# A two-layer graph attention kernel: transposes of the layer input in odd steps, layer-0 sums counted behind V, mask tiles of the first batch turned inside the stream

## Chip, cores and metric

The kernel runs on one core of one Trainium2 chip. The metric is the device time of one execution in microseconds, as the median of several runs.

## What is computed

`x` is 16 x 1024 x 256 in float32, `adj` is 16 x 1024 x 1024 in int32 (0 or 1). Two layers follow each other, each a pre-norm graph attention with a residual; layer 0 has 4 heads of 64, layer 1 has 8 heads of 32 and biases. Cut to what matters:

```python
for layer in (0, 1):                       # H = 4, then 8; D = 256 // H
    h = relu(layernorm(x))
    q, k, v = h @ Wq, h @ Wk, h @ Wv       # per head; layer 1 with bq, bk, bv
    s = q @ k.T / sqrt(D)                  # per batch and head, 1024 x 1024
    s = where(adj, s, -inf)
    x = x + concat_heads(softmax(s) @ v) @ Wo + bo
```

## The kernel before

All matmuls are float32. Keys lie on the 128 partitions of a score tile and 512 queries on its columns. A *group* is one batch, one layer, one half of the queries (`qh`) and one half of the heads (`g`: 2 heads in layer 0, 4 in layer 1). A *step* makes four 128x512 score blocks of a group: two key tiles of two heads in layer 0 (4 steps a group), one key tile of four heads in layer 1 (8 steps a group). A batch so has 16 layer-0 steps and 32 layer-1 steps.

All steps of all batches form one list, and layer 0 of batch b+1 stands ahead of layer 1 of batch b. In step i of this list (`Stream.run`, L436) TensorE gets the scores of step i (`scores`, L356, into two PSUM pairs `ps`), then the products with V of step i-2 (`weigh`, L389, into `po`; `LEAD` is 2). VectorE sets masked scores to a large negative number (L380) and ScalarE takes the exponential (L385). The pool `ps_s` has three PSUM pairs; a step's scores take two of them in turn, and every projection, transpose or output product takes one.

The sums of the exponentials come from a matmul with ones (`count`, L268, into `pz`). In layer 1 GpSimd first adds the tiles of two steps (L482) and the count is put into step i+2. In layer 0 VectorE and GpSimd add the tiles of a group (`add_tiles`, L401) and one count follows at its end. Then `spread` (L285) copies the sums out of PSUM on ScalarE and re-lays them by two DMAs through DRAM (`sd`, `sn`), `invert` (L294) takes the reciprocal on VectorE and brings it back broadcast (`vd`, `inv`), `test` (L306) checks the range of the sums on GpSimd, `normalize` (L313) multiplies on GpSimd, and `end_half` (L340) multiplies with Wo and adds to x.

The inputs of the next layers are made in between, in pieces placed by hand: `later(i, f)` puts a function into step i, `due` holds them, and they are issued at the end of the step in the order in which they were entered. The pieces are `stats` and `norm` (mean and variance on VectorE, normalized rows `hn` on ScalarE), `add_bias`, `turn` (L189, eight TensorE transposes of `hn` to `hT`), and `k`, `q`, `values`. `k`, `q`, `values` and `end_half` are the *large* units (L428). An even step that has a large unit holds its products with V back, and the next odd step does those of both.

The mask of a batch comes in eight tiles: `load` (GpSimd's DMA queue, which also turns int32 to bf16), `flip` (SyncE's transposing DMA), `put` (ScalarE, to fp8), with two buffers before and two behind the flip. The second layer's form of the mask is made in place by `second` (L136, VectorE). In the first batch all eight tiles are put ahead of the stream. SyncE's queue (SP) issues all other DMAs in program order.

For the batches in the middle, with a the first layer-0 step of a 48-step cycle and c = a+16 its first layer-1 step, the placing is (each named unit for one half of 512 rows):

| unit | before |
|---|---|
| k, q, v and k of the coming layer-1 batch | a+2, a+4, a+6, a+8 |
| its remaining v and q | c+2, c+4 |
| turns of the coming layer-1 batch | c+28, c+30 |
| turn, k, q, v of the next layer-0 batch, half 0 | a+14, c+6, c+10, c+12 |
| the same, half 1 | c+14, c+16, c+18, c+20 |
| output products of layer 0 | c, c+8 |
| output products of layer 1 | c+26, a+10 |

Of the kernel before, what the change touches and what calls it, by code (L numbers as in the profile page):

```python
# [18 lines left out]
P = 128  # L19
# [3 lines left out]
LEAD = 2  # L23

# [15 lines left out]
def load_weights(nc, const, a):  # L40
# [19 lines left out]
    for layer in range(2):  # L60
        for kind, mats in (("k", w.k), ("q", w.q), ("v", w.v), ("o", w.o)):
            mats.append(mat(a[f"w{kind}{layer}"], f"w{kind}{layer}"))
# [3 lines left out]
    w.bv = col(a["bv1"], "bv1")  # L66
    w.ident = const.tile([P, P], F32, tag="ident", name="ident")
# [8 lines left out]
def fast_program(ctx, tc, a, w, loads, chk):  # L76
# [26 lines left out]

    bo = [w.bo[0]]
# [39 lines left out]
    class Inputs:  # L144
# [37 lines left out]
        def add_bias(self, half):  # L182

            rows = xs[self.b, half]
            nc.gpsimd.tensor_add(
                rows, rows, bo[self.layer].unsqueeze(1).to_broadcast([P, 4, E])
            )
# [58 lines left out]
    class Group:  # L246
# [21 lines left out]
        def count(self, p, start, stop):  # L268
# [3 lines left out]
            for r in range(self.per):  # L272
# [3 lines left out]
                )  # L276

# [93 lines left out]
    def exponentials(st, between):  # L371
# [5 lines left out]
        for i in range(2):  # L377
# [8 lines left out]
            if i == 0:  # L386
                between()
# [32 lines left out]
    class Stream:  # L420
# [7 lines left out]
        def large(self, i):  # L428
            return any(
                f.__name__ in ("k", "q", "values", "end_half") for f, _ in self.due.get(i, [])  # L430
            )

        def later(self, i, f, *args):
            self.due.setdefault(i, []).append((f, args))

        def run(self):  # L436
# [3 lines left out]
            for i in range(n + LEAD):  # L440
# [5 lines left out]
                copy = lambda: None  # L446
                if i % 2 or not self.large(i):
                    for st in waiting:
                        weigh(st)
                    for st in waiting:  # L450
                        if st.gr.layer:
                            self.count_steps(i, st)
                        if st.last:
                            copy = st.gr.copy_out
                            self.end_group(i, st.gr)
                    waiting = []
                if now:
                    exponentials(now, copy)
                else:
                    copy()  # L460
# [3 lines left out]
                for f, args in self.due.pop(i, []):  # L464
                    f(*args)
# [25 lines left out]
        def end_group(self, i, gr):  # L491

            if gr.layer == 0:
                i += 1
                self.later(i, gr.count, gr.t, True, True)
            elif not gr.hurry:
                i += 2
            self.later(i, gr.spread)
            if gr.hurry:
                self.later(i, gr.finish)  # L500
                self.later(i, gr.test)
                return
            self.later(i + 2, gr.invert)
            self.later(i + 3, gr.test)

            self.later(i + (5 if gr.layer and not gr.last else 4), gr.normalize)
            if gr.g == 1:
                self.later(i + (7 if gr.layer else 6), gr.end_half)
# [19 lines left out]
    def tiles(*ts):  # L528
        for t in ts:
            mask.flip(t)  # L530
            (mask if t + 2 < NT else masks[1]).load((t + 2) % NT)
            open_w(-(-len(loads) // 2))

    tiles(0, 1)
# [62 lines left out]
    for t in range(NT):  # L597
        later(2 * t, masks[1].flip, t)
        later(2 * t + 1, masks[1].put, t)
# [296 lines left out]
```

## Time and profile before

| | |
|---|---|
| median of 3 runs | 3406.17 us (3405.55 to 3406.78) |
| profiled execution | 3402.26 us, its span 3400.5 us |
| granted TensorE clock | 0.996 of full speed |
| busy: PE, DVE, ACT, POOL | 3359.3, 2468.8, 2188.1, 2446.0 us |
| scores L364, V L396, count L273 | 1167.4, 989.9 and 267.8 us of PE |
| masking L380, exponentials L385 | 1801.3 us of DVE, 1618.2 us of ACT |
| layer-1 tile adds L482 | 1163.0 us of POOL |
| DMA | 141.76 MB, 42 GB/s in the mean |

Busy times of engines run side by side, so they do not add up to the span. A TensorE row of the timeline joins the matmuls of one line; its second column runs to a modelled end, and the distance from the start of one row to the start of the next says how long TensorE really spent on it.

### The profile page before, as it was taken

How to read it: one execution, taken by the hardware profiler on the slowest of the kernel's cores; microseconds unless marked ns; L12 is line 12 of the kernel's file. 1: busy time of each engine (PE TensorE's matmuls, PEld its weight loads, DVE VectorE, ACT ScalarE, POOL GpSimd, SP SyncE). 2: the span in 40 equal slices, each digit the busy share in tenths (PEclk: the TensorE clock that was granted, in tenths of full speed). 3: DMA queues.
4: the chain of work that ended last, by engine and by line, in shares of the span. 5: the costliest groups of instructions: out<-in, count | busy, mean ns of one | idle time of the engine just before them, and what ended most of it. 6: DMA issues, size and time to landing. Idle time of an engine off the chain costs nothing. (4 is left out here: it accounts for less than half of the span.)

```text
span 3400.5 us, 46245 instructions
## 1 busy us (share of the span) xinstructions
PE 3359.3 (99%) x18190; PEld 1302.6 (38%) x18190; DVE 2468.8 (73%) x2664; ACT 2188.1 (64%) x2402; POOL 2446.0 (72%) x1606
## 2 busy tenths in 40 slices
PE   7999999999999999999999999999999999999998
PEld 3443343433434333343333334334343343433432
DVE  4676767777677776777767777677776777767876
ACT  5566666676666756667566675666756667565665
POOL 4577777777777776777668686686867768677777
PEclk9999999999999999999999999999999999999999
DMA  6212121211212122121111212112122111210001
GB/s 133 44 36 36 47 42 36 49 37 47 40 36 51 34 49 36 36 51 42 42 35 39 48 42 45 34 43 45 39 48 39 42 41 41 47 35 23 14 17 31
DMA packets 250737, 141.76 MB, mean 42 GB/s; under 512 B 182416, under 2 KB 217488, under 8 KB 250512
## 3 DMA queue, kind: packets, MB, share of 16 engines
q1 hardware_dynamic: 232080, 105.18, 12.6%
q0 software_dynamic: 18432, 33.56, 6.4%
q8 instruction: 144, 2.36, 0.3%
q14 instruction: 81, 0.66, 0.1%
HBM read 120.33 MB, written 18.34 MB: 41 GB/s over the span
## 5 line engine op out<-in xcount | busy, mean ns | idle before, releaser
L380 DVE SCALAR_TENSOR_TENSOR p<-mask,ps 128x1024 f32<-128x1024 fp8e4 x1536 | 1801.3, 1215 | 753.7 <-PE ps L364 729.1
L385 ACT ACTIVATE p<-p 128x1024 f32<-128x1024 f32 x1536 | 1618.2, 1057 | 984.1 <-DVE p L380 940.9
L482 POOL TENSOR_TENSOR p<-p,p 128x2048 f32<-128x2048 f32 x255 | 1163.0, 4562 | 399.9 <-PE po L396 396.1
L364 PE MATMUL ps<-qT,kT 32*128 32x512 f32 (+1 forms) x6144 | 1167.4, 633 | 13.1 <-DVE p L380 8.7
L396 PE MATMUL po<-p,v 128*32 128x512 f32 (+1 forms) x6144 | 989.9, 601 | 0.5 <-ACT o L280 0.5
L409 POOL TENSOR_TENSOR t<-t,t 128x1024 f32<-128x1024 f32 x192 | 479.1, 2495 | 401.3 <-DVE t L407 324.4
L364 PEld LDWEIGHTS ps<-qT,kT 32*128 32x128 f32 (+1 forms) x6144 | 375.0, 184 | 726.2 <-issue 364.0
L396 PEld LDWEIGHTS po<-p,v 128*32 128x32 f32 (+1 forms) x6144 | 229.1, 118 | 688.3 <-issue 529.3
L407 DVE TENSOR_TENSOR t<-p 128x1024 f32<-128x1024 f32 x192 | 292.7, 1525 | 0.9
L273 PE MATMUL pz<-p,ones 128*32 128x512 f32 x2056 | 267.8, 593 | 0.2 <-POOL p L482 0.2
L207 PE MATMUL pq<-hT,wk 128*128 128x512 f32 x512 | 240.0, 612 | 2.7 <-ACT hT L196 2.6
L236 PE MATMUL pv<-wv,hT 128*128 128x256 f32 x1024 | 237.9, 385 | 0.0
L345 PE MATMUL py<-wo,cat 128*128 128x256 f32 x1008 | 234.2, 385 | 2.5 <-DVE p L380 2.5
L207 PE MATMUL pq<-hT,wq 128*128 128x512 f32 x512 | 236.6, 605 | 0.0
L236 PEld LDWEIGHTS pv<-wv,hT 128*128 128x128 f32 x1024 | 189.4, 190 | 70.7 <-issue 36.1
L345 PEld LDWEIGHTS py<-wo,cat 128*128 128x128 f32 x1008 | 186.4, 190 | 73.2 <-issue 32.3
L316 POOL TENSOR_TENSOR cat<-o,inv 128x512 f32<-128x512 f32 x127 | 164.3, 1294 | 20.7 <-DMA inv<-vd 14.7
L407 POOL TENSOR_TENSOR t<-p 128x1024 f32<-128x1024 f32 x64 | 171.5, 2680 | 0.4
L131 ACT ACTIVATE mask<-adjT,mhalf 128x1024 fp8e4<-128x1024 bf16 x128 | 145.5, 1138 | 10.1 <-DMA adjT<-adj 10.1
L207 PEld LDWEIGHTS pq<-hT,wk 128*128 128x128 f32 x512 | 93.3, 192 | 144.3 <-issue 137.1
L207 PEld LDWEIGHTS pq<-hT,wq 128*128 128x128 f32 x512 | 92.1, 189 | 139.8 <-issue 128.5
L177 ACT ACTIVATE hn<-x,shift,rstd 128x256 f32<-128x256 f32 x256 | 138.1, 588 | 6.9 <-POOL shift L170 6.9
(52 smaller groups left out, 1567.8 us busy)
## 6 DMA issues: line engine op xcount, KB each, us to landing
adj<-in_adj_dram POOLq DMA_DIRECT2D x128, 256.0 KB, 3.6
x<-in_x_dram SPq DMA_DIRECT2D x32, 512.0 KB
inv<-vd SPq DMA_DIRECT2D x128, 128.0 KB
inv<-vd SPq DMA_DIRECT2D x252, 64.0 KB
out_dram<-x SPq DMA_DIRECT2D x31, 512.0 KB
adjT<-adj SPq DMA_TRANSPOSE x128
sd<-s SPq DMA_DIRECT2D x64, 4.0 KB
sn<-sd SPq DMA_DIRECT2D x64, 4.0 KB
```

The lines of the kernel that those rows point to most:

```text
L207: nc.tensor.matmul(pq[:, m, :], wt[self.layer][:, c, ts(m, P)], self.hT[half][:, c, :], start=(c == 0), stop=(c == 1),)
L236: nc.tensor.matmul(pv[:, i, :], self.hT[half][:, c, ts(i, P)], w.v[self.layer][:, c, :], start=(c == 0), stop=(c == 1),)
L273: nc.tensor.matmul(self.s[r * self.D : (r + 1) * self.D, :], w.ones[:, : self.D], p[:, r, :], start=start, stop=stop,)
L316: nc.gpsimd.tensor_mul(self.half.cat[:, self.g, :], self.ob, self.inv)
L345: nc.tensor.matmul(py[:, i, :], self.half.cat[:, c, ts(i, P)], w.o[self.layer][:, c, :], start=(c == 0), stop=(c == 1),)
L364: nc.tensor.matmul(st.ps[i // 2][:, i % 2, :], gr.inp.kT[r * D : (r + 1) * D, gr.g, ts(kt, P)], gr.inp.qT[r * D : (r + 1) * D, gr.g, ts(gr ...
L380: nc.vector.scalar_tensor_tensor(out=half, in0=gr.mask.m[:, kt, ts(gr.qh, 512)].unsqueeze(1).to_broadcast([P, 2, 512]), scalar=BIG, in1=st ...
L385: nc.scalar.activation(half, half, AF.Exp, scale=gr.scale)
L396: nc.tensor.matmul(gr.o[r * D : (r + 1) * D, :], gr.inp.v[:, kt, h * D : (h + 1) * D], st.p[:, i, :], start=(kt == 0), stop=(kt == NT - 1),)
L407: engine.tensor_add(t, st.p[:, 0:2, :], st.p[:, 2:4, :])
L409: nc.gpsimd.tensor_add(t, t, gr.t)
L482: nc.gpsimd.tensor_add(one, one, st.p)
```

## The change

- `turn` of the layer inputs goes from even to odd steps wherever layer 1 is running (c+14 to c+15, c+28 to c+27, c+30 to c+29).
- Counts are issued directly behind the products with V, ahead of the step's other units. The layer-0 count and `spread` are due one step later than before, `invert` stays, and for a batch's last layer-1 group `invert`, `normalize` and `end_half` come one, two and one steps earlier.
- Units due in one step are sorted: small ones first, turns and large units last.
- Large units are placed anew: v and q of the coming layer-1 batch at c+4 and c+6; k, q, v of the next layer-0 batch at c+10, c+12, c+14 (half 0) and c+18, c+20, c+24 (half 1); the second layer-1 output product at a+9.
- The prologue puts four mask tiles of the first batch; the other four, and then those of batch 1, are flipped and put one per step, from steps 1 and 2 on.
- x of batch 1 is loaded between the first mask tiles; x of later batches, half 1, at a+10 for a+11. Weights of layer 1 are loaded after those of layer 0 and the biases.
- The product of bv and Wo (`pb`) moves from the prologue to step 9 and is added in place to the bias row, which also serves the second program (taken only where a sum leaves its range).

```diff
@@ -22,6 +22,9 @@
 LEAD = 2
+LARGE = ("k", "q", "values", "end_half")
+COUNTS = ("count", "count_added")
 SUM_MIN, SUM_MAX = 1e-15, 1e15
@@ -57,13 +60,17 @@
         return t
     w.k, w.q, w.v, w.o = [], [], [], []
-    for layer in range(2):
-        for kind, mats in (("k", w.k), ("q", w.q), ("v", w.v), ("o", w.o)):
-            mats.append(mat(a[f"w{kind}{layer}"], f"w{kind}{layer}"))
+    def mats(layer):
+        for kind, of in (("k", w.k), ("q", w.q), ("v", w.v), ("o", w.o)):
+            of.append(mat(a[f"w{kind}{layer}"], f"w{kind}{layer}"))
+    mats(0)
     w.bo = [row(a["bo0"], "bo0"), row(a["bo1"], "bo1")]
     w.bq = col(a["bq1"], "bq1")
     w.bk = col(a["bk1"], "bk1")
     w.bv = col(a["bv1"], "bv1")
+    mats(1)
     w.ident = const.tile([P, P], F32, tag="ident", name="ident")
     make_identity(nc, w.ident)
     w.ones = const.tile([P, 64], F32, tag="ones", name="ones")
@@ -275,6 +280,9 @@
                     start=start, stop=stop,
                 )
+        def count_added(self):
+            self.count(self.t, True, True)
         def copy_out(self):
             self.ob = work.tile([P, 512], F32, tag="o", name=f"o_{self.n}")
             nc.scalar.copy(self.ob, self.o)
@@ -427,11 +436,15 @@
         def large(self, i):
             return any(
-                f.__name__ in ("k", "q", "values", "end_half") for f, _ in self.due.get(i, [])
+                f.__name__ in LARGE for f, _ in self.due.get(i, [])
             )
         def later(self, i, f, *args):
             self.due.setdefault(i, []).append((f, args))
+        def rank(self, entry):
+            return entry[0].__name__ in ("turn", *LARGE)
         def run(self):
             steps = self.steps
@@ -443,7 +456,7 @@
                     waiting.append(steps[i - LEAD])
                 if now:
                     scores(now)
-                copy = lambda: None
+                copies = []
                 if i % 2 or not self.large(i):
                     for st in waiting:
                         weigh(st)
@@ -451,18 +464,25 @@
                         if st.gr.layer:
                             self.count_steps(i, st)
                         if st.last:
-                            copy = st.gr.copy_out
+                            copies.append(st.gr.copy_out)
                             self.end_group(i, st.gr)
                     waiting = []
+                due = self.due.pop(i, [])
+                for f, args in due:
+                    if f.__name__ in COUNTS:
+                        f(*args)
                 if now:
-                    exponentials(now, copy)
+                    exponentials(now, copies)
                 else:
-                    copy()
+                    for f in copies:
+                        f()
                 one = steps[i - 1] if 1 <= i <= n else None
                 if one and one.gr.layer == 0:
                     add_tiles(one)
-                for f, args in self.due.pop(i, []):
-                    f(*args)
+                for f, args in sorted(due, key=self.rank):
+                    if f.__name__ not in COUNTS:
+                        f(*args)
             while self.due:
                 for f, args in self.due.pop(min(self.due)):
                     f(*args)
@@ -490,22 +510,21 @@
         def end_group(self, i, gr):
+            if gr.hurry:
+                for f in (gr.spread, gr.finish, gr.test):
+                    self.later(i, f)
+                return
             if gr.layer == 0:
-                i += 1
-                self.later(i, gr.count, gr.t, True, True)
-            elif not gr.hurry:
-                i += 2
-            self.later(i, gr.spread)
-            if gr.hurry:
-                self.later(i, gr.finish)
-                self.later(i, gr.test)
-                return
-            self.later(i + 2, gr.invert)
-            self.later(i + 3, gr.test)
-            self.later(i + (5 if gr.layer and not gr.last else 4), gr.normalize)
+                self.later(i + 2, gr.count_added)
+                at = 2, 3, 5, 7
+            else:
+                at = (2, 3, 4, 8) if gr.last else (2, 4, 7, 9)
+            for k, f in zip(at, (gr.spread, gr.invert, gr.normalize)):
+                self.later(i + k, f)
+            self.later(i + at[1] + 1, gr.test)
             if gr.g == 1:
-                self.later(i + (7 if gr.layer else 6), gr.end_half)
+                self.later(i + at[3], gr.end_half)
     def open_w(n):
         for _ in range(n):
@@ -525,46 +544,48 @@
     inp.stats(1)
     inp.turn(0)
-    def tiles(*ts):
-        for t in ts:
-            mask.flip(t)
-            (mask if t + 2 < NT else masks[1]).load((t + 2) % NT)
-            open_w(-(-len(loads) // 2))
-    tiles(0, 1)
+    def flip(u):
+        masks[u // NT].flip(u % NT)
+        if u + 2 < 2 * NT:
+            masks[(u + 2) // NT].load((u + 2) % NT)
+    def put(u):
+        masks[u // NT].put(u % NT)
+    flip(0)
+    flip(1)
+    open_w(1)
     inp.k(0)
     inp.norm(1)
     inp.q(0)
     inp.turn(1)
-    mask.put(0)
-    mask.put(1)
+    put(0)
+    put(1)
     inp.values(0)
-    tiles(2, 3)
+    flip(2)
+    open_x(1, 0)
+    flip(3)
+    open_w(5)
+    open_x(1, 1)
     inp.k(1)
-    mask.put(2)
-    mask.put(3)
-    tiles(4, 5)
+    put(2)
+    put(3)
     inp.q(1)
-    mask.put(4)
-    mask.put(5)
-    tiles(6, 7)
     inp.values(1)
-    mask.put(6)
-    mask.put(7)
+    open_w(len(loads))
     for half in range(QH):
-        open_x(1, half)
         inp.add_bias(half)
-    pb = psum_pair("pb")[:, 0, :E]
-    for c in range(2):
-        nc.tensor.matmul(
-            pb, w.bv[:, c : c + 1].to_broadcast([P, P]), w.o[1][:, c, :],
-            start=(c == 0), stop=(c == 1),
-        )
-    bo1 = small.tile([P, E], F32, tag="bo1", bufs=1, name="bo1v")
-    nc.vector.tensor_add(bo1, pb, w.bo[1])
-    bo.append(bo1)
+    def bias_of_v():
+        pb = psum_pair("pb")[:, 0, :E]
+        for c in range(2):
+            nc.tensor.matmul(
+                pb, w.bv[:, c : c + 1].to_broadcast([P, P]), w.o[1][:, c, :],
+                start=(c == 0), stop=(c == 1),
+            )
+        nc.vector.tensor_add(w.bo[1], pb, w.bo[1])
@@ -580,13 +601,11 @@
     stream = Stream(steps)
     later = stream.later
-    def norms(inp, half, i):
-        later(i, inp.stats, half, (0, 1))
-        later(i + 1, inp.stats, half, (2, 3))
-        later(i + 3, inp.norm, half, (0, 1))
-        later(i + 4, inp.norm, half, (2, 3))
-        later(i + 5, inp.add_bias, half)
+    def norms(inp, half, *at):
+        for i, f in zip(at, (inp.stats, inp.stats, inp.norm, inp.norm)):
+            later(i, f, half, (0, 1) if i in (at[0], at[2]) else (2, 3))
+        later(at[3] + 1, inp.add_bias, half)
     def half_inputs(inp, half, *at):
@@ -594,49 +613,48 @@
             later(i, f, half)
-    for t in range(NT):
-        later(2 * t, masks[1].flip, t)
-        later(2 * t + 1, masks[1].put, t)
-        if t + 2 < NT:
-            later(2 * t + 1, masks[1].load, t + 2)
-    for half in range(QH):
-        norms(inputs[0][1], half, 3 * half)
+    for u in range(4, 2 * NT):
+        later(u - 3, flip, u)
+        later(u - 2, put, u)
+    later(9, bias_of_v)
+    norms(inputs[0][1], 0, 0, 1, 3, 4)
     half_inputs(inputs[0][1], 0, 5, 6, 8, 10)
+    norms(inputs[0][1], 1, 3, 4, 6, 7)
     half_inputs(inputs[0][1], 1, 11, 12, 14, 16)
     for b in range(B - 1):
         mine, a, c = inputs[1][b], first[b + 1], second[b]
         if b == 0:
-            norms(mine, 0, a + 1)
-            norms(mine, 1, a + 9)
+            norms(mine, 0, a + 1, a + 2, a + 4, a + 5)
             half_inputs(mine, 0, a + 6, a + 8, a + 10, a + 12)
-            half_inputs(mine, 1, a + 15, c, c + 4, c + 2)
+            norms(mine, 1, a + 9, a + 10, a + 12, a + 13)
+            half_inputs(mine, 1, a + 15, c + 2, c + 6, c + 4)
         else:
-            norms(mine, 0, a - 10)
-            norms(mine, 1, a - 8)
-            half_inputs(mine, 0, a - 4, a + 2, a + 4, a + 6)
-            half_inputs(mine, 1, a - 2, a + 8, c + 4, c + 2)
+            norms(mine, 0, a - 10, a - 9, a - 7, a - 6)
+            half_inputs(mine, 0, a - 5, a + 2, a + 4, a + 6)
+            norms(mine, 1, a - 8, a - 7, a - 5, a - 4)
+            half_inputs(mine, 1, a - 3, a + 8, c + 6, c + 4)
         for kt in range(NT):
             later(a + 4 + kt, masks[b].second, kt)
         if b + 2 < B:
             other, mask = inputs[0][b + 2], masks[b + 2]
             later(a + 1, open_x, b + 2, 0)
-            later(a + 11, open_x, b + 2, 1)
-            norms(other, 0, a + 7)
-            norms(other, 1, a + 15)
-            half_inputs(other, 0, a + 14, c + 6, c + 10, c + 12)
-            half_inputs(other, 1, c + 14, c + 16, c + 18, c + 20)
+            later(a + 10, open_x, b + 2, 1)
+            norms(other, 0, a + 7, a + 8, a + 10, a + 11)
+            half_inputs(other, 0, a + 14, c + 10, c + 12, c + 14)
+            norms(other, 1, a + 15, c + 1, c + 3, c + 4)
+            half_inputs(other, 1, c + 15, c + 18, c + 20, c + 24)
             for t in range(NT):
                 i = a + 2 + 5 * t
                 later(i, mask.load, t)
                 later(i + 3, mask.flip, t)
                 later(i + 5, mask.put, t)
         else:
-            last = inputs[1][b + 1]
-            norms(last, 0, c + 1)
-            norms(last, 1, c + 9)
-            half_inputs(last, 0, c + 6, c + 10, c + 12, c + 14)
-            half_inputs(last, 1, c + 16, c + 20, c + 36, c + 34)
+            last, e = inputs[1][b + 1], c + 32
+            norms(last, 0, c + 1, c + 2, c + 4, c + 5)
+            half_inputs(last, 0, c + 9, c + 12, c + 14, c + 16)
+            norms(last, 1, c + 9, c + 10, c + 12, c + 13)
+            half_inputs(last, 1, c + 17, c + 20, e + 6, e + 4)
             for kt in range(NT):
                 later(c + 8 + 2 * kt, masks[b + 1].second, kt)
     stream.run()
...
```

More of the change, by code (lines that the diff above doesn't have):

```diff
@@ L102, in psum_pair @@
         return ps_s.tile([P, 2, 512], F32, tag="ps_s", name=name)
-    bo = [w.bo[0]]
     xs = {}
@@ L185, in add_bias @@
             nc.gpsimd.tensor_add(
-                rows, rows, bo[self.layer].unsqueeze(1).to_broadcast([P, 4, E])
+                rows, rows, w.bo[self.layer].unsqueeze(1).to_broadcast([P, 4, E])
             )
@@ L386, in exponentials @@
             if i == 0:
-                between()
+                for f in between:
+                    f()
     def weigh(st):
@@ L453, in run @@
                         if st.last:
-                            copy = st.gr.copy_out
+                            copies.append(st.gr.copy_out)
                             self.end_group(i, st.gr)
                     waiting = []
+                due = self.due.pop(i, [])
+                for f, args in due:
+                    if f.__name__ in COUNTS:
+                        f(*args)
                 if now:
-                    exponentials(now, copy)
+                    exponentials(now, copies)
                 else:
-                    copy()
+                    for f in copies:
+                        f()
                 one = steps[i - 1] if 1 <= i <= n else None
@@ L665, in careful_program @@
     actp = ctx.enter_context(tc.tile_pool(name="cact", bufs=1))
-    bv = actp.tile([P, E], F32, tag="bv", name="c_bv")
-    nc.sync.dma_start(bv, a["bv1"].partition_broadcast(P))
     work = ctx.enter_context(tc.tile_pool(name="cwork", bufs=2))
@@ L706, in layer_of @@
                 )
-            if layer == 0:
-                nc.scalar.copy(v[:, t, :], pv)
-            else:
-                nc.vector.tensor_add(v[:, t, :], pv, bv)
+            nc.scalar.copy(v[:, t, :], pv)
         for half in range(N // 512):
```

## Prediction

> **What bounds the kernel now.** I read the page's busy shares first, then TensorE's timeline in the start and in one batch, then VectorE's and ScalarE's beside it.
>
> ```profile
> PE 3359.3 (99%) x18190; PEld 1302.6 (38%) x18190; DVE 2468.8 (73%) x2664; ACT 2188.1 (64%) x2402; POOL 2446.0 (72%) x1606
> ```
>
> TensorE (PE) bounds the span, but is 99% "nothing left"? By that row only 41 us of the 3400.5 could ever be won. The Trainium skill (Perfetto Trace Analysis, "Identifying the Most-Contended Engine") says that matmul busy time does not measure the distance to the peak, because matmuls are pipelined. The timeline decides:
>
> ```profile
> 26.54 3.60 PE L207 MATMUL pq<-hT,wk 128*128 128x512 f32 x8
> 29.97 3.60 PE L207 MATMUL pq<-hT,wq 128*128 128x512 f32 x8
> 33.41 3.62 PE L236 MATMUL pv<-wv,hT 128*128 128x256 f32 x16
> ```
>
> From start to start eight such instructions take 3.43 us, 0.43 us each (half for 256 columns, a half or a quarter where two or four tiles of the array run side by side). With that price all matmuls of the trace sum to 2951 us. I went through the 1930 runs of equal matmuls and took from each start-to-start time this price: 325 us are switches (0.03 to 0.24 us for each pair of kinds, the same every time), and 109 us are waits. So the rule holds, and waits can be won inside "busy" PE. They lie in three places.
>
> The start (PE, then ScalarE):
>
> ```profile
> 37.82 1.13 PE L364 MATMUL ps<-qT,kT 64*128 64x512 f32 x4
> 41.40 6.76 PE L364 MATMUL ps<-qT,kT 64*128 64x512 f32 x16 [2.46 <-ACT v L240]
> 54.29 2.08 PE L364 MATMUL ps<-qT,kT 64*128 64x512 f32 x4 [6.12 <-DVE p L380]
> 56.30 2.68 PE L396 MATMUL po<-p,v 128*64 128x512 f32 x8
> ...
> 47.68 1.15 ACT L131 ACTIVATE mask<-adjT,mhalf 128x1024 fp8e4<-128x1024 bf16 x1 [0.96 <-DMA adjT<-adj]
> 48.74 1.99 ACT L385 ACTIVATE p<-p 128x1024 f32<-128x1024 f32 x2
> ```
>
> ScalarE stands in order behind the eighth mask tile (47.68); the first exponentials (48.74) wait for it, though they need no tile after the fourth. Three steps of scores are issued, then PE waits: 37.82 to 56.30 for 5.3 us of work.
>
> Layer 1, batch 5, steps c+22 to c+26 (a cycle has 48 steps: a is its first layer-0 step, c = a+16 its first layer-1 step):
>
> ```profile
> 1368.34 1.06 PE L396 MATMUL po<-p,v 128*32 128x512 f32 x8
> 1369.33 1.51 PE L364 MATMUL ps<-qT,kT 32*128 32x512 f32 x8
> ...
> 1372.63 1.55 PE L364 MATMUL ps<-qT,kT 32*128 32x512 f32 x8
> 1374.11 1.06 PE L396 MATMUL po<-p,v 128*32 128x512 f32 x8
> 1375.10 2.39 PE L364 MATMUL ps<-qT,kT 32*128 32x512 f32 x8
> ```
> ```profile
> 1368.44 2.35 DVE L380 SCALAR_TENSOR_TENSOR p<-mask,ps 128x1024 f32<-128x1024 fp8e4 x2 [1.20 <-PE ps L364]
> 1370.71 0.42 DVE L160 BATCH_NORM_STATS2 st<-x 128x6 f32<-128x256 f32 x1
> ```
>
> A scores block takes 1.07 us to the next start. Behind an even step with no large unit it takes 1.44 (1369.33 to 1370.77): its second half needs the PSUM pair that the first masking of c+22 frees about 1369.6. Behind c+24, also empty, with two statistics pairs of 1.2 us in VectorE's way, it takes 2.33. In batches 1 to 13 these waits repeat to 0.03 us: c+1 0.73, c+15 0.48, c+23 0.37, c+24 0.41, c+25 1.25, c+26 0.48, c+29 0.48, c+31 0.48, together 4.68 of a period of 209.4. c+15, c+29 and c+31 follow a turn in an even step: the turn (1.02 us) takes the third PSUM pair and is too short to cover both maskings.
>
> **The change part by part.**
>
> *Start.* Only four mask tiles are put before the stream; flips and puts 4 to 15 go one per step, `pb` goes to step 9 (its 0.96 us moves, gains nothing). Scores of step 0 start when V of half 1 ends, about 36.7; masking about 37.9 to 40.2, exponentials to 41.3. Statistics of steps 0 and 1 (now in VectorE's way, 1.2 us each) push the masking of step 1 to about 42.6, scores of step 2 end about 43.7, V(0) about 45.6. Before, the same point (scores of step 3) is at 58.90: 13.3 saved. PE's granted clock, 0.69 in the window 38 to 60, stays up as a result; that is within the 13.3. Two later waits in step 2 (0.74) and at step 6 (1.58, hT late because the put before it waited for its transpose) I count as 1.0 saved.
> What the moved steps queue: the transpose DMAs stand on SP, each mask load on POOL right behind the flip whose buffer it needs, the puts on ScalarE behind the exponentials. A load takes 3.65 us to land, flip issue to landing about 3.6 (25.37 to the load released at 28.95), so with two buffers a tile per 4.2 us; steps take 3.8 to 5.5, and tiles 4 and 5 are in hand before step 2. POOL may stand up to 3 us for a load in steps 3 to 6; waiting behind it are the adds of `t`, wanted by the counts two steps later. If the cover is gone, each put delays a step by the missing 1 to 3 us. The second x is issued on SP between flips 2 and 3, 512 KB beside them, which I let delay put 3 by up to 3 us; it is ready at 33.3, needed at 37.9.
>
> *Layer-1 waits.* Turns move from c+14, c+28, c+30 to c+15, c+27, c+29, behind V and count (1.07+0.88+0.97 us, so both maskings are past). V of half 1 fills c+24, so the waits of c+25 and c+26 (1.73) go. Units still number eleven on 16 even steps; c+2, c+16, c+22, c+28, c+30 are empty afterwards. What is late next is the scores behind each: c+3 0.43, c+17 0.37, c+23 0.37, c+24 0.41 (statistics stay there), c+29 0.37, c+31 0.50 (hT's copy behind two hn of 0.59 on ScalarE frees the pair late). Sum 2.45. The wait of c+1 goes because the count leaves step a+14, so a+15's scores and masking run 1.0 us earlier, against a wait of 0.73. Saved 4.68-2.45 = 2.2 a batch; over 14 batches (first one 3.95 before) 30.5.
> Last two batches: 21 us of waits, 5.4 of them at c+20 of batch 14, where a second-mask op of VectorE ran 4.42 us beside POOL's 4.53 us add. With c+16 filled, POOL's add ends first. I take 4 saved; bounds 0 and 7.
>
> *Order on PE.* By the trace's switch prices: V to layer-0 count 0.06, V to scores 0.16-0.17, projection (pv, py) to count or scores 0.24, turn to either 0.17. 64 layer-0 counts go from behind turns and units to behind V: 64 x 0.11 = 7 saved. `end_half` moves from a+10 to a+9, so V of step a+8 no longer joins the next: 14 more V runs, about 0.2 each, 2.8 paid. Turn behind a count is in no row: 0.12 as count to scores, 0.03 to 0.24 at most, x44 = +-4. Net 4.5 saved.
>
> *Waits added.* The layer-0 count and with it `spread` come one step later, `invert` stays: VectorE's reciprocal now follows one step behind the copy of the sums, as it does for the last layer-1 group (invert a+4 for a+5, normalize a+5 for a+7). Behind it on VectorE stands the next masking, and PE waits for that. The row first: in batch 5 `sd` is issued at 1329.23 and `sn`, which waits for its landing, at 1330.97; over all 128 pairs the median from the end of the copy to the issue of `sn` is 1.71 us. Two such hops are 3.4, under the shortest layer-0 step of 3.79. The skill (DMA: Bandwidth & Descriptors, "Anatomy of one DMA") speaks against the change: a fixed cost of about 2.0 us per DMA, mostly the write receipt and longest into HBM (stated for the path from GpSimd; these two go from SP). That makes 4.0, plus issue 0.5 and copy 0.6, so over the step. By it the reciprocal waits 1 us, five places a batch; yet VectorE can be about 2 us late in layer 0 before a scores block lacks its pair (a masking pair is 2.35 us, a step 3.79). By both I charge 0; bounds 0 and 0.5 x 80 = 40. `normalize` on POOL may wait 1 us for `inv`; the steps a+5 to a+9 (23 us) cover it. `out` and the next x follow at a+9 and a+10: SP waits for the store, and nothing else of SP is due before a+11.
>
> Sum: 14.3 + 30.5 + 4 + 4.5 = 53 us. The profiled execution took 3402.3 (span 3400.5 and 1.8 around it) and would take 3349; the median of the runs is 3406.2, 3.9 above the profiled one, so I forecast 3353.
>
> **Rivals.**
> 1. *Waits only move* (0.12): five even steps remain empty. If c+1 stays and two more 0.7 us waits appear per batch, layer 1 gains nearly nothing: 53-30 = 23, 3383. For it: the count of units is unchanged. Against: the 1.25 and 0.48 at c+25 and c+26 come from the empty c+24, which is filled.
> 2. *The start gives back half* (0.13): puts wait for their transposes in steps 2 to 6, five times 1.5 us: 3361.
> 3. *Slower* (0.06): `sn` lands so late that the reciprocal holds VectorE in layer 0 and at a+4. 80 places; it decides from 0.67 us of PE time each (53/80), which is a round trip over about 6.5 us (step 3.8, slack 2, plus 0.67). At 0.85 us each the time is 3421. For it: SP is one queue, and a flip or store wait can stand before `sd`. Against: 2.69 us is the longest first hop in 128.
> 4. *No effect* (0.03): start and layer 1 cancel against new waits. That the order does not change is excluded: the program as built has the layer-0 counts behind V and the turns at odd steps.
>
> **How the numbers follow.** Forecast 0.66, within 3336 to 3368 (mask locks, turn price, and start +-5). The range reaches to rivals 1 and 2: 3336 to 3383. A measurement here tells about 0.2%, 6.8 us, from no change. Faster by more: 0.66+0.12+0.13 less a rest, 0.90; within: 0.03; slower: 0.07.
>
> **What would show it.** First V at about 43 to 45 instead of 56.3; a batch period of about 206.9 instead of 209.4; scores at c+25 and c+26 back at 1.07; 0.37 to 0.5 at c+3, c+17, c+29, c+31; reciprocals without a wait on `sn`. A wait of VectorE for `sn` over 2 us, or a period above 208.5, would make it wrong.

## The result and the profile after

The changed kernel takes 3377.75 us in the median (3376.91 to 3380.06, 4 runs) against 3405.86 us (3402.88 to 3406.78, 4 runs) for the kernel before: a ratio of 0.992, 95% interval 0.9903 to 0.9937. It is 28.1 us faster, 0.53 of the 53 us forecast. The time lies inside the stated range of 3336 to 3383, which reached to two rivals, and outside the 3336 to 3368 that the prediction gave its own mechanism. The profiled execution took 3380.06 us, its span 3378.3 us.

The share of busy time on its page says as little as before (TensorE, weight loads, VectorE, ScalarE, GpSimd):

```profile
PE 3339.0 (99%) x18190; PEld 1298.6 (38%) x18190; DVE 2501.1 (74%) x2664; ACT 2182.5 (65%) x2402; POOL 2447.1 (72%) x1606
```

VectorE has the same 2664 instructions and is busy 32 us longer. That is the one hint on the page; the group of the page that grew is shown below.

*The start*, TensorE's timeline, answering to the four rows from 37.82 on (start, length to a modelled end, engine, line, operation, idle before and its releaser):

```profile
43.58 1.13 PE L372 MATMUL ps<-qT,kT 64*128 64x512 f32 x4 [1.06 <-DVE p L388]
44.64 1.94 PE L405 MATMUL po<-p,v 128*64 128x512 f32 x8
...
56.54 1.13 PE L372 MATMUL ps<-qT,kT 64*128 64x512 f32 x4 [1.34 <-DVE p L388]
...
65.51 5.40 PE L212 MATMUL pq<-hT,wk 128*128 128x512 f32 x8 [2.04 <-ACT hT L201]
```

The first V begins at 44.64 instead of 56.30, as forecast (43 to 45). Then the scores of step 5 wait (56.54), as they did not before, and the first K of the second half waits 2.04 us for `hT` (65.51), where it waited 1.51 before. That K takes 5.40 us; the K and Q of the prologue took 3.60.

*Layer 1, batch 5, c+22 to c+26*, TensorE, answering to the rows from 1368.34 on:

```profile
1352.80 1.51 PE L372 MATMUL ps<-qT,kT 32*128 32x512 f32 x8
...
1356.09 1.55 PE L372 MATMUL ps<-qT,kT 32*128 32x512 f32 x8
1357.64 3.72 PE L241 MATMUL pv<-wv,hT 128*128 128x256 f32 x16
1361.29 1.14 PE L372 MATMUL ps<-qT,kT 32*128 32x512 f32 x8
...
1365.08 1.14 PE L372 MATMUL ps<-qT,kT 32*128 32x512 f32 x8
```

The scores at c+25 (1361.29) and c+26 (1365.08) are back at 1.07 us to the next start; before, c+25 took 2.33. c+24 (1356.09) keeps 0.48 of waiting.

*The seam of layer 0 and layer 1*, steps c and c+1 of the same batch, TensorE and then VectorE with GpSimd:

```profile
1259.84 1.14 PE L372 MATMUL ps<-qT,kT 32*128 32x512 f32 x8
1260.91 0.70 PE L353 MATMUL py<-wo,cat 128*128 128x256 f32 x2
1261.84 3.29 PE L353 MATMUL py<-wo,cat 128*128 128x256 f32 x14 [0.23 <-POOL cat L324]
1265.12 2.26 PE L372 MATMUL ps<-qT,kT 32*128 32x512 f32 x8
1267.31 3.65 PE L405 MATMUL po<-p,v 128*64 128x512 f32 x16
```
```profile
1253.84 3.39 DVE L416 TENSOR_TENSOR t<-p 128x1024 f32<-128x1024 f32 x1
...
1260.60 2.27 DVE L416 TENSOR_TENSOR t<-p 128x1024 f32<-128x1024 f32 x1 [1.12 <-POOL t L418]
1262.80 0.41 DVE L165 BATCH_NORM_STATS2 st<-x 128x6 f32<-128x256 f32 x1
...
1263.87 2.32 DVE L388 SCALAR_TENSOR_TENSOR p<-mask,ps 128x1024 f32<-128x1024 fp8e4 x2
```
```profile
1250.79 2.38 POOL L190 TENSOR_TENSOR x<-x,bo 128x1024 f32<-128x1024 f32 x1
...
1253.76 2.37 POOL L416 TENSOR_TENSOR t<-p 128x1024 f32<-128x1024 f32 x1
...
1260.52 1.27 POOL L324 TENSOR_TENSOR cat<-o,inv 128x512 f32<-128x512 f32 x1
```

Here is what the forecast lost. Scores of c+1 take 2.19 us to the next start (1265.12 to 1267.31) instead of 1.07: a wait of 1.12, where 0.73 stood before and 0 was forecast. The output product at c is broken in two, 0.54 of waiting that is new. Behind them, VectorE's addition to `t` takes 3.39 us instead of 1.22. It starts 0.08 us behind an addition of GpSimd and ends 1.10 us behind that one's end (1256.13). The next one waits 1.12 for the `t` that GpSimd still holds, meets `cat`, and takes 2.27. Two different things then come late. GpSimd ends `cat` at 1261.79, and the third matmul of the output product, which needs it, starts at 1261.84: this is the wait at c. VectorE begins the statistics and the maskings of step c (1263.87) late, and the second half of the scores of c+1 starts at 1266.25, when the second of these maskings has ended (1266.19) and its PSUM pair is free: this is the wait at c+1.

From batch 1's first layer-1 scores to batch 13's, a cycle is 208.38 us in the mean (before 209.41, forecast 206.9). TensorE's waits in it, in us:

| step | before | forecast | after |
|---|---|---|---|
| c | 0 | 0 | 0.54 |
| c+1 | 0.73 | 0 | 1.12 |
| c+3, c+17, c+23, c+31 | 0, 0, 0.37, 0.48 | 0.43, 0.37, 0.37, 0.50 | 0.37 each |
| c+24 | 0.41 | 0.41 | 0.48 |
| c+25, c+26, c+15 | 1.25, 0.48, 0.48 | 0 | 0 |
| c+28, c+29 | 0, 0.48 | 0, 0.37 | 0.23, 0.14 |
| sum | 4.68 | 2.45 | 4.0 |

### The profile page after: what moved, and what is told of

Its sections match the earlier page's. It is cut to its first block, busy times and chain, and to the rows that moved or that the text cites. A ratio compares the mean times of both kernels' runs of the same rounds, so it can differ in the third digit from the quotient of the medians.

```text
span 3378.3 us, 46298 instructions
## 1 busy us (share of the span) xinstructions
PE 3339.0 (99%) x18190; PEld 1298.6 (38%) x18190; DVE 2501.1 (74%) x2664; ACT 2182.5 (65%) x2402; POOL 2447.1 (72%) x1606
## 5 line engine op out<-in xcount | busy, mean ns | idle before, releaser
L372 PE MATMUL ps<-qT,kT 32*128 32x512 f32 (+1 forms) x6144 | 1145.6, 631 | 7.6 <-DVE p L388 4.9
L418 POOL TENSOR_TENSOR t<-t,t 128x1024 f32<-128x1024 f32 x192 | 486.2, 2532 | 389.8 <-DVE t L416 341.6
L372 PEld LDWEIGHTS ps<-qT,kT 32*128 32x128 f32 (+1 forms) x6144 | 367.7, 184 | 675.7 <-issue 305.3
L416 DVE TENSOR_TENSOR t<-p 128x1024 f32<-128x1024 f32 x192 | 325.0, 1693 | 14.6 <-POOL t L418 14.4
L358 DVE TENSOR_TENSOR x<-py,x 128x1024 f32<-128x1024 f32 x63 | 76.4, 1213 | 118.4 <-PE py L353 118.4
L190 POOL TENSOR_TENSOR x<-x,bo 128x1024 f32<-128x1024 f32 x64 | 152.6, 2385 | 1.5 <-DMA bo<-in_bo_dram 1.4
```

Source lines behind the costliest of these rows:

```text
L372: nc.tensor.matmul(st.ps[i // 2][:, i % 2, :], gr.inp.kT[r * D : (r + 1) * D, gr.g, ts(kt, P)], gr.inp.qT[r * D : (r + 1) * D, gr.g, ts(gr ...
L416: engine.tensor_add(t, st.p[:, 0:2, :], st.p[:, 2:4, :])
L418: nc.gpsimd.tensor_add(t, t, gr.t)
```

## The experiments

"Cycle" is that mean period in the profiled execution of each kernel, "step 16" the start of that step's scores. Each group was timed beside the kernel before on the same chip.

### e1_out_a10: the last output product one step later again

```diff
-                at = (2, 3, 4, 8) if gr.last else (2, 4, 7, 9)
+                at = (2, 3, 4, 9) if gr.last else (2, 4, 7, 9)
...
-            later(a + 10, open_x, b + 2, 1)
+            later(a + 11, open_x, b + 2, 1)
```

> The changed kernel with the last layer-1 output product back at a+10 (and the x load behind it at a+11). In the changed kernel six steps in a row (a+10 to a+15) have no large unit, and TensorE then waits 0.54 us at c and 1.12 us at c+1. Theory A (VectorE and GpSimd fall behind in this run of six): with the product in the middle of it the waits at c and c+1 fall to 0.7 us or less together, a cycle takes about 207.2 to 207.6 us against 208.36, and the whole 3362 to 3367 against 3378. Theory B (the later count and spread are what makes c late): the waits stay at 1.6 us and the cycle within 0.3 us of 208.36.

3364.07 us (3363.38 to 3364.48), ratio 0.9876 (0.986 to 0.9893); cycle 207.38. The wait at c is gone, that at c+1 is 0.79. Moving `end_half` from a+10 to a+9 had left a+10 to a+15 without a large unit; this one step costs 1.0 us a cycle, of which 0.2 was charged.

### e2_count_old: the layer-0 count one step after the last V, as before

```diff
-                self.later(i + 2, gr.count_added)
+                self.later(i + 1, gr.count_spread)
```

`count_spread` counts and spreads at the end of the step.

> The changed kernel with layer-0 count and spread where they were before: one step after the last V, at the end of the step behind turn and large units. Theory B (later count and spread make c late): the waits at c and c+1 fall to 0.7 us or less, less 0.4 us a cycle for the lost switches (0.11 us for each of four counts): about 207.7. Theory A (run of six steps): the waits at c and c+1 stay at about 1.1 to 1.7 us in all, and the switches cost 0.4 us: a cycle of 208.4 to 208.8, the whole 3378 to 3385.

3385.62 us (3381.7 to 3385.83), ratio 0.9936 (0.9919 to 0.9952); cycle 208.62. c+1 keeps its 1.12: the later count does not make it. The wait at c falls to 0.37, that at c+3 goes, and 0.45 appears at c+4; net, the count behind V is worth 0.24 us a cycle. The whole is 7.9 us slower than the changed kernel, of which the cycles explain 3.4; in the profiles batch 14 takes 3.0 more (124.8 us for 121.8 from its first layer-1 scores to batch 15's).

### e3_stats_c1: the statistics of the next layer-0 batch's second half later

```diff
-            norms(other, 1, a + 15, c + 1, c + 3, c + 4)
+            norms(other, 1, c + 1, c + 2, c + 4, c + 5)
```

> The changed kernel with the statistics of the second half of the next layer-0 input at c+1 and c+2 (norm at c+4 and c+5) in place of a+15 and c+1: 1.2 us of VectorE leave the stretch ahead of the first masking of c. If the waits at c and c+1 are VectorE's lateness, c+1 falls from 1.12 to about 0.1 to 0.5 and c stays at 0.54 (it waits for something ahead of it), the cycle takes about 207.5 to 207.8 and the whole 3366 to 3371. If the transpose or the PSUM pair of the output product sets the wait, nothing changes (within 0.2 us of 208.36).

3368.31 us (3367.56 to 3369.19), ratio 0.9888 (0.9872 to 0.9905); cycle 207.61. c+1 falls to 0.11, c keeps 0.5, and 0.32 appears at c+4. So 1.2 us of statistics ahead of the masking of c set the wait at c+1, but not that at c, which is for `cat` here too (it ends at 1255.13, the product goes on at 1255.19).

### e4_load_later: the mask loads of the first two batches one step behind their flips

```diff
+    def flip_alone(u):
+        masks[u // NT].flip(u % NT)
...
-        later(u - 3, flip, u)
+        later(u - 3, flip_alone, u)
         later(u - 2, put, u)
+        later(u - 2, load_next, u)
```

> The changed kernel with the mask loads of the first two batches one step later than the flip whose buffer they need, so that GpSimd does not stand in front of a transpose. In the changed kernel TensorE waits 9 us in steps 2 to 6 of the first batch. Theory P (GpSimd's stand for the loads makes its adds collide with VectorE's): the waits of steps 5 and 6 (1.6, 1.0, 2.1, and 1.7 at a lower granted clock) fall to 3 us or less, 3 to 5 us off the whole (3373 to 3375), nothing in later cycles. Theory Q (statistics and mask tiles are simply too much for VectorE and ScalarE in these steps): within 1 us of the changed kernel's start (step 16 at 125 us).

3382.49 us (3379.96 to 3382.96), ratio 0.9928 (0.9912 to 0.9945); step 16 at 125.2, as in the changed kernel. The wait of step 5 at VectorE's masking goes (VectorE's addition ahead of it takes 1.36 us instead of 3.02), and the turn then waits 3.54 us for `hn`. So loads standing on GpSimd have a part in step 5's wait, but taking them away did not make the start shorter; why `hn` comes late then was not tested. In the profiles batch 14 also takes 3.3 us more than in the changed kernel.

### e5_both: e1_out_a10 and e3_stats_c1 together

> The changed kernel with both: output product at a+10 again, and the statistics at c+1 and c+2. Each alone took 1.0 and 0.77 us off a cycle of 208.38; what remained of them was 0.79 us at c+1 in the one, 0.5 at c and 0.3 at c+4 in the other. If both act on one lateness of VectorE at the entry of layer 1, together they take what was left, not their sum: a cycle of 206.6 to 206.9 us, the whole 3354 to 3358. If they are independent: 206.6 or less as well, with no wait at c+4; if the one merely hides the other: 207.4, 3364.

3357.59 us (3357.24 to 3358.39), ratio 0.986 (0.9844 to 0.9877); cycle 206.87. Both waits go, 0.32 stays at c+4. Together the edits take 1.51 us off a cycle, against 1.00 and 0.77 alone: they add in the main, and the cycle is the forecast's 206.9.

### e6_start_alone: the kernel before with the new prologue only

```diff
-    tiles(0, 1)
+    flip(0)
+    flip(1)
+    open_w(1)
...
-    tiles(4, 5)
     inp.q(1)
-    mask.put(4)
-    mask.put(5)
-    tiles(6, 7)
     inp.values(1)
-    mask.put(6)
-    mask.put(7)
```

> The kernel before with the new start alone (four tiles ahead, the others one per step, x of batch 1 sooner, weights in the new order, the product of bv in step 9); large units, turns and counts as before. The recorded forecast has 14 us for it; the changed kernel's trace shows 12.4 us at step 3 and 7.7 at the first layer-1 step. If the loss of 5 us belongs to the start, this kernel is 7 to 11 us faster than before (3395 to 3399); if it belonged to the new order of units and counts, it is 13 to 15 us faster (3391 to 3393). Later cycles stay at 209.4 us.

3394.63 us (3394.13 to 3397.13), ratio 0.9968 (0.9956 to 0.9981). The start alone is worth 10.7 us, against 14.3 forecast. Its profile has nearly the same waits in steps 5 and 6 (1.04 and 2.04 us), so the start makes its own loss.

### e7_v24_alone: the kernel before with one V moved

```diff
-            half_inputs(other, 1, c + 14, c + 16, c + 18, c + 20)
+            half_inputs(other, 1, c + 14, c + 16, c + 18, c + 24)
```

> The kernel before with one unit moved: V of half 1 of the next layer-0 batch at c+24 for c+20. By the forecast's step the waits at c+25 (1.25) and c+26 (0.48) go and the wait behind an empty even step comes at c+21 (0.37): a cycle of 208.0 to 208.1 us against 209.4 and a whole of 3387 to 3389. If the statistics only move the wait to c+27 and later, the cycle stays within 0.4 us of 209.4.

3386.82 us (3386.59 to 3387.24), ratio 0.9946 (0.9929 to 0.9962); cycle 208.13. The waits of c+25 and c+26 go, 0.37 appears at c+21. This one number in one line is worth 18.5 us. With the start's 10.7 that is 29.2, all that the whole change brings (28.1). The turns in odd steps, the counts and the other places together net nothing as they stand: what they gain is given back at c and c+1.

### e8_bias_c8: one addition of GpSimd away from the seam

```diff
-            norms(other, 0, a + 7, a + 8, a + 10, a + 11)
+            norms(other, 0, a + 7, a + 8, a + 10, a + 11, bias=c + 8)
```

`add_bias` of that half, L190 in the seam above, goes from a+12 to c+8; all else is the changed kernel.

> The changed kernel with GpSimd's bias add of the next layer-0 batch (2.4 us) at c+8 in place of a+12, inside the run of six steps without a large unit. In the changed kernel VectorE's add of a+14 takes 3.39 us instead of 1.22 because it starts when GpSimd's adds do. If GpSimd's lateness is what makes VectorE late at c: that row falls to 1.3 to 2.4 us, the waits at c and c+1 from 1.66 to under 0.9, a cycle of 207.3 to 207.7. If VectorE is late by its own work (statistics, mask, maskings), the cycle stays at 208.2 to 208.5.

3357.37 us (3355.87 to 3357.63), ratio 0.9859 (0.9843 to 0.9876); cycle 206.76, the forecast's 206.9 within 0.14. The same steps in its timeline, TensorE, VectorE and GpSimd:

```profile
1249.56 1.14 PE L372 MATMUL ps<-qT,kT 32*128 32x512 f32 x8
1250.63 3.72 PE L353 MATMUL py<-wo,cat 128*128 128x256 f32 x16
1254.28 1.14 PE L372 MATMUL ps<-qT,kT 32*128 32x512 f32 x8
1255.35 3.65 PE L405 MATMUL po<-p,v 128*64 128x512 f32 x16
```
```profile
1243.55 1.22 DVE L416 TENSOR_TENSOR t<-p 128x1024 f32<-128x1024 f32 x1
...
1248.36 2.05 DVE L416 TENSOR_TENSOR t<-p 128x1024 f32<-128x1024 f32 x1
```
```profile
1241.14 2.38 POOL L416 TENSOR_TENSOR t<-p 128x1024 f32<-128x1024 f32 x1
```

GpSimd's addition now ends (1243.52) as VectorE's begins (1243.55). That one is back at 1.22 us, the next no longer waits for `t`, `cat` ends at 1249.33, ahead of the output product, which is whole, and the scores of c+1 take 1.07. The page's group of these additions, first in the changed kernel and then in this one (busy, mean ns, idle before and releasers):

```profile
L416 DVE TENSOR_TENSOR t<-p 128x1024 f32<-128x1024 f32 x192 | 325.0, 1693 | 14.6 <-POOL t L418 14.4
```
```profile
L416 DVE TENSOR_TENSOR t<-p 128x1024 f32<-128x1024 f32 x192 | 293.2, 1527 | 0.3 <-POOL t L418 0.2
```

The 32 us that VectorE was busy longer are these 192 additions (before 292.7), and 14 us of waiting for `t` come on top. GpSimd is no less busy in this kernel (2447.3 us); only its order changed, and by the medians the kernel is 20.4 us faster than the changed one.

### e9_stats_early, e10_first_stats, e11_seconds, e12_all: what else is left

On the kernel of e8_bias_c8:

```diff
-            norms(mine, 0, a - 10, a - 9, a - 7, a - 6)
+            norms(mine, 0, a - 20, a - 19, a - 7, a - 6)
...
-            norms(mine, 1, a - 8, a - 7, a - 5, a - 4)
+            norms(mine, 1, a - 14, a - 13, a - 5, a - 4)
```

> The kernel of e8_bias_c8 with the statistics of the coming layer-1 batch eight (first half) and six (second half) steps earlier: steps c+12, c+13 and c+18, c+19 of the cycle in place of c+22 to c+25; its normalizing and turning steps stay. If the 0.48 us that TensorE still waits at step c+24 in each cycle is VectorE giving the evictions of that step late because of these statistics, that wait goes: 0.48 us x 14 cycles = 6.7 us, the cycle 206.2 to 206.4 us in place of 206.76, the whole 3349 to 3352 us. If the wait is set by the V unit's own place among the matmuls, or the statistics only collide with something else at their new steps, the cycle stays at 206.6 to 206.9 us and the whole at 3355 to 3359 us.

3351.66 us (3347.91 to 3352.35), ratio 0.9841 (0.9824 to 0.9857); cycle 206.24. TensorE at c+24 and behind it:

```profile
1341.66 1.14 PE L372 MATMUL ps<-qT,kT 32*128 32x512 f32 x8
1342.73 3.72 PE L241 MATMUL pv<-wv,hT 128*128 128x256 f32 x16
```

1.07 us between them instead of 1.55: the wait of c+24 was the statistics'.

```diff
-    norms(inputs[0][1], 1, 3, 4, 6, 7)
+    norms(inputs[0][1], 1, 7, 8, 9, 10)
```

> The kernel of e8_bias_c8 with the first batch's second-half statistics at steps 7 and 8 and its normalizing at 9 and 10, in place of 3, 4, 6 and 7. If the start gives back part of what the prologue gains because these statistics and the masks of the first steps want VectorE at the same time, the waits of steps 5 and 6 (1.6 and 2.1 us in the profile of the changed kernel) shrink, the scores of step 16 begin at 117 to 119 us in place of 121.2, and the whole falls by 2 to 4 us to 3353 to 3356 us. If ScalarE's copies of hT, put behind its exponentials, set it, nothing moves: 3356 to 3359 us. The start has come out at two values about 4 us apart in equal kernels, so it is read from the rows of steps 2 to 8 and not from the whole alone.

3356.05 us (3355.23 to 3357.31), ratio 0.9855 (0.9839 to 0.9872); step 16 at 121.5, against 121.2. The K of the second half still waits 1.63 us for the copy of hT on ScalarE. The scores of step 0 began 1.4 us later in this execution, so about 1.1 us may have been gained on the way; the timed runs can't tell it from nothing.

```diff
-            for kt in range(NT):
-                later(c + 8 + 2 * kt, masks[b + 1].second, kt)
+            for kt, k in enumerate((4, 6, 8, 12, 14, 16, 20, 26)):
+                later(c + k, masks[b + 1].second, kt)
```

> The kernel of e8_bias_c8 with the second masking operations of the last batch's masks, which run on VectorE in batch 14, moved from the even steps c+8 to c+22 to steps c+4, 6, 8, 12, 14, 16, 20 and 26. If the waits of batch 14 (3.30 + 1.70 us at c+20) come from such an operation standing on VectorE behind GpSimd's addition to p in the step of a large unit, moving it takes 4 to 6 us away: the stretch from batch 14's first scores to batch 15's falls from 123.5 to 118 to 120 us and the whole to 3351 to 3354 us. If any place gives one such collision, the wait reappears at another step of batch 14 and the whole stays at 3355 to 3360 us.

3350.49 us (3349.68 to 3351.24), ratio 0.9841 (0.9824 to 0.9857); from batch 14's first scores to batch 15's 117.9 us instead of 123.5. The waits at c+20 were the second masking operation's.

All three:

> The three edits of e9_stats_early, e10_first_stats and e11_seconds together on e8_bias_c8. If each removes its own wait they add: 6.7 + 3 + 5 = some 14 us, 3341 to 3347 us. If two of them share a cause or one only moves its wait, the whole is 3347 to 3354 us.

3342.14 us (3341.8 to 3343.15), ratio 0.9815 (0.9799 to 0.9831), with a cycle of 206.24 and 117.9 in batch 14: the gains add. It is 35.6 us faster than the changed kernel and 63.2 us faster than the kernel before.

## Why the prediction was half right

By its own terms, against the profiled execution, whose span fell by 22.2 us of the 53:

| term | forecast | in the profile |
|---|---|---|
| start, up to batch 0's first layer-1 scores | 14.3 | 7.7 |
| waits of layer 1 and order on PE, up to batch 14 | 35.0 | 15.6 |
| last two batches and end | 4 | -1.1 |

**"The wait of c+1 goes" is the step that failed.** 1.12 and 0.54 per cycle where 0 was written, 1.66 x 13 = 21.6 us up to batch 14, against the 19.4 missing in that row (some other waits came out smaller). The step let the moved count run a+15's scores earlier, and took VectorE and GpSimd to keep their times. The count is not what decides: with it back in its place c+1 still waits 1.12 (e2_count_old). Taking `end_half` out of a+10 left six short steps in a row, and TensorE ran ahead of both. GpSimd's work up to c stayed the same, more of it now fell upon VectorE's additions, and each such meeting made VectorE wait out GpSimd's instruction. That `end_half` moved was seen in the forecast, but only its 0.2 us switch was costed. e1_out_a10 (undo it), e3_stats_c1 (give VectorE less there) and e8_bias_c8 (give GpSimd less there) each take waits away, and e8_bias_c8 and e5_both give the forecast's cycle (206.76 and 206.87). No other place of the layer-1 sum was off by more than 0.23. The forecast's sign for failure was a cycle over 208.5; 208.38 is just under it, and far from 206.9. That the time stayed inside the stated range is owed to the range's width, which was drawn for other causes.

The Trainium skill has the rule that would have priced this (SBUF — State Buffer, "SBUF: two separate sides"): VectorE and GpSimd have one pair of SBUF ports in common, an exclusive lock that whoever starts first holds for its whole instruction; a VectorE operation with two SBUF inputs takes part in it against a GpSimd operation that reads SBUF. The rows agree. The addition to `t`, with two such inputs, takes 1.22 us alone; begun 0.08 behind GpSimd's 2.37 it takes 3.39, which is that one's remainder and 1.10. It works the other way too: GpSimd's next small comparison (L318, 128x8), 0.26 us alone, takes 1.12 and ends just behind VectorE's addition, in all 13 places where it begins during one. A pair of maskings, with one input from PSUM, takes 2.35 us beside GpSimd's 4.56 us addition as elsewhere. The kernel before had such rows too (2.60 us for this addition in the same batch, with GpSimd's at its side), and they were not read.

**The start's first half was right.** 12.4 us are saved at the scores of step 3 (58.90 to 46.51) for 13.3. The "later 1.0" was wrong in sign: by step 16 5.4 are given back. VectorE's addition in step 4 meets GpSimd's:

```profile
51.29 3.02 DVE L416 TENSOR_TENSOR t<-p 128x1024 f32<-128x1024 f32 x1
```
```profile
50.86 2.36 POOL L418 TENSOR_TENSOR t<-t,t 128x1024 f32<-128x1024 f32 x1
```

It ends 1.09 behind GpSimd's end, and 1.07 us of statistics stand behind it; so step 5 waits 1.34 (no such wait in e4_load_later and e8_bias_c8, where that addition takes 1.36 and 1.35). Then ScalarE's copy of hT, behind exponentials, lets K wait 2.04, and the granted clock falls. In the table by stretches the columns are stretch, length, busy time (and instructions) of PE, PEld, DVE, ACT and POOL, granted clock, DMA share and GB/s:

```profile
65.50:71.00 5.50, 5.49 (x10) 2.18 (x12) 0.65 (x1) 3.93 (x6) 5.47 (x4) 0.69 0.54 92
```

At that clock the eight matmuls of K take 1.7 us more (5.40 us, against 3.70 in e8_bias_c8). This execution was the dearest of its four; by medians the start is worth 10.7 (e6_start_alone), and in the profile of e8_bias_c8, which has the same start, 11.7 (batch 0's first layer-1 scores at 212.49 for 224.18).

**The order on PE was right.** 209.41 - 208.38 = 1.03 a cycle, of which the waits explain 0.68; 0.35 x 14 = 4.9 us for 4.5 forecast (the prediction's own terms, 7 less 2.8, make 4.2).

**The last batches.** 4 us were taken because a filled c+16 would let GpSimd end first. It did not:

```profile
3212.40 3.96 DVE L144 TENSOR_SCALAR mask<-mask 128x1024 fp8e4<-128x1024 fp8e4 x1
```
```profile
3211.27 4.54 POOL L502 TENSOR_TENSOR p<-p,p 128x2048 f32<-128x2048 f32 x1 [0.24 <-PE po L405]
```

The operation, 0.68 us alone, ends 0.55 after GpSimd's: the same pattern as with the additions, though it has one SBUF input; why it takes part is not shown. Batch 14 saves 1.3 us and the end is 2.4 longer, of which 1.3 is the last output product: 4.98 us instead of 3.69, with the granted clock at 0.50 from 3363.4 to 3366.8. On top of e8_bias_c8, e11_seconds moves these operations and takes 5.6 us off batch 14.

**Waits added, charged 0: right in time, wrong in the sign to look for.** VectorE does wait for `sn`, in every batch behind the scores of c+5 (engine, line, awaited: us in total, times, longest):

```profile
DVE vn L305 <- DMA sn<-sd: 43.5, 22, 3.5
```
```profile
1282.45 0.20 DVE L305 RECIPROCAL vn<-sn 128x8 f32<-128x8 f32 x1 [2.52 <-DMA sn<-sd]
```

The prediction called a wait over 2 us a proof against it. TensorE loses nothing: V of c+4 is running, and its next scores and products come without a gap. The two hops take 3.20 us (`sd` issued at 1279.25), so the 3.4 read from the row was nearer than the 4.0 that the prediction worked out from the Trainium skill's fixed cost per DMA.

**The rivals.** In layer 1 the case that came nearest is "waits only move" (c+1 stays, one new wait beside it), with 0.12. "The start gives back half" has its size in the profiled execution but not its cause: no put waited for its transpose (they begin at 48.97, 52.37 and 58.61 without idle time). "Slower" fell, since the waits for `sn` cost TensorE nothing, and "no effect" is outside the interval.

## What to carry to other kernels

When a change lets the bounding engine run ahead, go through the helpers' order at each seam where large work no longer stands between: it is their lateness, not their share of busy time, that ends the wait. Look for instructions of VectorE and GpSimd that begin together; one whose length varies in the trace (1.22 and 3.39 us for the same shape) marked such a meeting here, and moving one off cost nothing (e8_bias_c8). Test each part of a large change alone: here two parts carried the whole gain, and the third needed one more edit to pay.

## What the hardware showed that was not expected

- How often the two engines hold each other up in a kernel that TensorE bounds: 58 of VectorE's 192 additions to `t` before, 73 after and 60 in e8_bias_c8 take over 1.5 us instead of 1.22, and every one of them ends 1.08 to 1.10 us behind a GpSimd instruction that it met. Of the 1536 maskings some 1400 run beside GpSimd in each kernel, and none takes over 1.22. The in-place fp8 operation on the mask is held up too (0.68 us alone, 3.96 in batch 14).
- Whether a wait of 2 us lowers the granted clock depends on where it falls. In the clock records of all fourteen traces the clock is 1.00 or 0.50 and changes at whole multiples of 3.41 us. In the changed kernel the stretch of 3.41 us that ends at 66.11 holds the whole 2.04 us wait of K, and the next one (66.12 to 69.53) runs at 0.50. In e8_bias_c8 the stretch that ends at 64.79 holds 1.81 of the same wait, and the clock stays at 1.00. Ahead of the last output product equal waits of 2.43 us lie in one stretch in the changed kernel (then 0.50) and in two, as 1.44 and 0.99, in the kernel before (1.00).
- The start is not the same in all executions: the scores of step 8 began at 77.2 to 77.4 us in three profiles (the changed kernel, e4_load_later, e6_start_alone) and at 73.2 to 74.3 in the nine others with the new prologue. In the three the clock fell once before step 8, which costs 1.7 us, and in none of the nine. In the changed kernel and e6_start_alone GpSimd had stood 2.42 and 2.12 us in step 4 for a mask tile's transpose, and VectorE's addition then met GpSimd's late one; in the seven fast ones that have their statistics in the same steps it stood 0.79 or less. What makes the transpose late stayed open.
